# A graph network on one core: what a gather waits for on TensorE, in the attention and at the two passages between layers

## The chip, the core and the metric

The kernel runs on one core of a Trainium2 chip. The metric is device time in microseconds (us) from start to end of one execution, lower is better. The core has four engines that compute (TensorE or PE, VectorE or DVE, ScalarE or ACT, GpSimd or POOL) and SyncE (SP), which issues most transfers. Each engine works through its own list of instructions in order, and waits on semaphores for the others.

## What is computed

A graph network over 6,250 nodes of 128 features and 200,000 edges that are sorted by their target node: two convolutions over the edges and then an attention over the edges. Norms, biases and the last residual are left out here:

```python
def mesh_conv(x, src, dst, ea, w1, b1, g, bt, w2, b2):
    m = jnp.concatenate([x[dst], x[src], ea], axis=-1) @ w1 + b1
    m = jax.nn.silu(group_norm(m, g, bt))
    m = m @ w2 + b2
    out = jax.ops.segment_sum(m, dst, num_segments=n)
    return out / jnp.clip(cnt, 1.0)[:, None]
...
h = mesh_conv(x, src, dst, edge_attr, c1_w1, ...)
...
h = mesh_conv(h, src, dst, edge_attr, c2_w1, ...)
...
q, k, v = h @ qw + qb, h @ kw + kb, h @ vw + vb
logits = (q[dst] * k[src]).sum(-1) * scale + (edge_attr @ ew + eb)
pe = jnp.exp(logits - segment_max(logits, dst)[dst])
w = pe / segment_sum(pe, dst)[dst]
o = jax.ops.segment_sum(w[:, :, None] * v[src], dst, num_segments=n)
```

Everything with `[dst]` is done with one-hot matrices on TensorE, because the edges are sorted by `dst`. Everything with `[src]` is a gather of rows from a table in DRAM.

## The kernel before

**Tiles and chunks.** 128 edges make a tile and TPC = 8 tiles a chunk; each of the three layers goes over NCH = 196 chunks, numbered here from 0 in the order of work (that is from the last nodes to the first; chunk 195 has three tiles). A gather (`indirect_dma_start` in `gather`, L796) is one instruction on POOL for one tile: it fetches 128 rows, of `b_d` in a convolution (128 numbers each), of `kv_d` in the attention (256 numbers, the key and the value). A chunk takes eight.

**The steps of a layer.** `pipeline` (L893) writes out step n of a layer. It fetches chunk n + 2 (`ahead` = 2): SP's loads of its node rows `pk` and of the indices `rel`, and POOL's eight gathers. Then it does the first half of chunk n and the second half of such earlier chunks as are due. In a convolution L1252 are the products of a chunk (TensorE), L1259 adds the gathered rows (DVE), and L1291 sums over the edges (TensorE). In the attention L1521 are the products `qe`, L1536 multiplies them with the gathered keys (DVE, where a chunk's logits begin), L1595 weights the gathered values (DVE, the last reader of a chunk's buffer), and L1602 sums. Logits are treated in runs: of four chunks first, then of eight. For a run of eight nothing but logits is done in the steps of its chunks; the maxima (L1569) and the weighting follow in the steps after. So chunks 4 to 11 are weighted from step 12 on, and in steps 8 to 11 there are logits alone.

**Buffers.** A convolution has four buffers for gathered rows. The attention has eleven, `gs`: three (`ge`) early ones, seven `g` and one `gl`; chunk c uses the buffer of chunk c - 11.

**What holds a gather.** Besides its buffer and its table, the first gather of a chunk may be held until TensorE has got to a place: `kept.seen` names the last TensorE instruction that had been written out when the chunk was fetched (`last_product`), and `held` makes the gather wait for it. In step n that is the last product of step n - 1, which in the attention are the products of chunk n. `fetched` leaves out the first fetch of a layer. In the attention that first fetch is chunk 2, which gathers nothing there, so chunk 3 is held:

```python
kept.seen = last_product() if fetched else None
new = ks[n + ahead] = stage.fetch(n + ahead)
kept.seen, fetched = None, True
```

**The passages between layers.** A layer's table is written by the layer before it, a batch of nodes at a time, and the last tile of nodes is ready only after the last edge sums (`last_tile`). The first EARLY = 3 chunks of convolution 2 and of the attention therefore gather from a copy (`b_e`, `kv_e`) that lacks this last tile. They do so while the layer before is still ending, and what they lack is added later with one-hot matrices `ohS` and the rows in `late` (L1700 and L1702 in the attention). Chunk 3 is the first that reads the complete table. In `last_tile` L972 are transpositions, L990 products and L1080 the stores of the last rows.

**Order on an engine.** DVE, SP, ACT and PE keep the order of the text, and POOL's gathers follow each other in the order in which they are written (`follows`). `ring` semaphores (`ring_r1` and so on) let the t-th gather of a chunk wait for the t-th of the chunk before.

Of the kernel before, what the change touches and what calls it, by code (L numbers as in the profile page):

```python
# [31 lines left out]
TPC = 8  # L32
# [6 lines left out]
EARLY = 3  # L39
# [18 lines left out]
def kernel(ctx: ExitStack, tc: tile.TileContext, x, src, dst, eat, w, out):  # L58
# [29 lines left out]
    kept = SimpleNamespace(h0=hpc.tile([P, NW, D], FP, name="h0"))  # L88
# [80 lines left out]
    b_d = {i: dram.tile([NW * P, D], FP, name=f"b_d{i}") for i in (1, 2)}  # L169
    kv_d = dram.tile([NW * P, KV], FP, name="kv_d")  # L170
    b_e = dram.tile([NW * P, D], FP, name="b_e")
    kv_e = dram.tile([NW * P, KV], FP, name="kv_e")
# [72 lines left out]
    with tc.tile_pool(name="node0", bufs=1) as np_, tc.tile_pool(name="prep", bufs=1) as pp, \  # L245
# [99 lines left out]
        back, firsts = sums[:, :NCH], sums[:, 2 * P:2 * P + NCH]  # L345
# [445 lines left out]
            tc.add_to_no_dep_group(key, h.ins)  # L791

    def gather(k, g, table_d, ring=None):
        n = k.nt
        for t in range(n):
            h = nc.gpsimd.indirect_dma_start(  # L796
                out=g[:, t, :table_d.shape[1]], out_offset=None, in_=table_d,
                in_offset=bass.IndirectOffsetOnAxis(ap=k.src[:, t:t + 1], axis=0))
            if ring is None:
                continue  # L800
            if kept.behind is not None:
                follows(h, kept.behind)
            kept.behind = h.ins
            if t == 0 and kept.seen is not None:
                held(h, kept.seen)
            ring.mark(h, k.at, t, n - 1)

    kept.behind = kept.seen = None

    def last_product():  # L810
        return next((i.name for i in reversed(nc.cur_bb.bb.instructions) if i.engine == mybir.EngineType.PE), None)

    def held(h, name):
        tc.add_manual_dep(
            h.ins, name, mybir.DependencyInfo(mybir.DependencyClass.Sync, mybir.DependencyReason.DATA),
            reason="held until TensorE is there")
# [76 lines left out]
    def pipeline(i, stage, following=None, aside=iter(()), then=iter(())):  # L893


        ends, todo = steps_of(i)
        starts = {n: j for j, (n, _, _) in enumerate(plans[i])}
        ahead = stage.ahead
        ks, under_way, said, fetched = stage.ks, [], {}, False

        def go_on(n, those):
            for g in those:
                if said.get(g) == "held" and n + 1 in ends:
                    continue
                said[g] = next(g, STOP)
                if said[g] is STOP:
                    under_way.remove(g)

        for c in range(ahead):
            if c not in ks:  # L910
                ks[c] = stage.fetch(c)
                compared(ks[c])
        stage.products(ks[0])
        for n, seconds in enumerate(todo):
            new = None
            if n + ahead < NCH and n + ahead not in ks:
                kept.seen = last_product() if fetched else None
                new = ks[n + ahead] = stage.fetch(n + ahead)
                kept.seen, fetched = None, True
            elif following and n + ahead >= NCH:  # L920
                kept.seen = last_product()
                new = following.prefetch(n + ahead - NCH)
                kept.seen = None
            if n + 1 < NCH and stage.soon:
                stage.products(ks[n + 1])
            run = [ks[c] for c in ends.get(n, ())]
            stage.root(run)
            early = stage.soon and n > NCH - SOON
            if early:
                ahead_of = [g for g in under_way if said.get(g) not in ("var", "root")]  # L930
                go_on(n, ahead_of)
            if new and stage.soon:
                compared(new)
            first = (lambda k: lambda: stage.first(k))(ks[n]) if n < NCH else None
            stage.then = [ks[c] for c in (todo[n + 1] if n + 1 < len(todo) else ()) if c in ks]
            if stage.second(run, [ks.pop(c) for c in seconds], first) and first:
                first()
            stage.finish()
            if new and not stage.soon:
                compared(new)  # L940
            if n + 1 < NCH and not stage.soon:
                stage.products(ks[n + 1])
            if n + 1 < len(todo):
                stage.early(ks, n, todo[n + 1])
            if n in starts:
                for _ in aside:
                    pass
                under_way.append(stage.batch(starts[n]))
            go_on(n, [g for g in under_way if not early or g not in ahead_of])
            if n > 4 and next(aside, STOP) is STOP and n > min(starts):  # L950
                next(then, None)
            if n < NCH:
                stage.reduce(ks[n])
        stage.flush()
        for g in (*under_way, aside, then):
            for _ in g:
                pass
# [206 lines left out]
    def nodes_of(b, i, w, m, hx=None):  # L1164
        return attention_nodes(b, w, m, hx) if i == 3 else conv_nodes(b, i, w, m, last=hx is not None)
# [22 lines left out]
    def last_tile(b, i, hx=True):  # L1188

        slots, b.bank = b.bank(), None  # L1190
        turn = itertools.cycle(range(BN))

        def slot():
            j = next(turn)
            return slots[:, j:j + 1, :]

        b.bank = slot
        b.var = lambda: last_var
        b.rs = last_rs
        nc.scalar.activation(last_sd[:, :1], eps_t, AF.Sqrt)  # L1200
        for r in nodes_of(b, i, 0, 1, hx):
            if r == "root":
                nc.scalar.activation(last_sd, last_var, AF.Sqrt, bias=eps_t, scale=1.0 / HD)  # L1203
            if r == ("inverse" if i == 3 else "root"):
                nc.vector.reciprocal(last_rs, last_sd)  # L1205
# [10 lines left out]
    def convs(general=False):  # L1216
        with ExitStack() as es:
            pool = lambda n, b, **kw: es.enter_context(tc.tile_pool(name=f"{n}{'g' if general else 'c'}", bufs=b, **kw))
            pools = {"oh": pool("oh", 2), "ps": pool("ps", 1, space=PSUM)}
            if not general:  # L1220
                pools["ohT"] = pool("ohT", 2)
                ring = Ring("ring", GB)
# [75 lines left out]

            class Stage:
                ahead, soon = 2, True  # L1300

                def __init__(self, i):
                    self.i, self.ks = i, {}
# [10 lines left out]
                def fetch(self, c):  # L1314
                    k = chunk(self.i, c)
                    loads(k, self.pools, a_d[self.i], wc_d[self.i])
                    k.g = gp.tile([P, TPC, D], FP, name="g")
                    gather(k, k.g, b_d[self.i] if k.ohS is None else b_e, ring)
                    k.h = hs[c % len(hs)]
                    return k  # L1320

# [144 lines left out]
    gs = [None] * (G + 3)  # L1466

    class AheadOfAttention:

        @staticmethod  # L1470
        def prefetch(c):
            k = chunk(3, c)
            gather(k, gs[c], kv_e, ring3)

    ahead_of = AheadOfAttention()

    def attention(general=False):
# [197 lines left out]

        class Stage:
            ahead, soon = 2, False
            sums, late, nb = [], [], None
            lg, j, both = None, 0, None

# [128 lines left out]
        if not general:  # L1809
            stage = Stage()  # L1810
# [127 lines left out]
```

## Time and profile before

| | |
|---|---|
| median of 3 runs | 6007.2 us (6005.33 to 6008.46) |
| the profiled execution | 6010.35 us, span 6008.6 us |
| convolution 1's gathers, from | 39.95 us |
| convolution 2's first early gather | 2002.8 us |
| the attention's first early gather | 3960.9 us |
| the attention's first gather of the complete table | 4011.5 us |
| the last gather | 5951.6 us |
| mean granted clock of TensorE | 0.746 |

The span goes from the first instruction to the last; the rest of an execution's time lies around it. In the rows of the timeline the first number is the start in us from the span's start, the second the duration; in brackets stands the idle time of the engine just before, and what ended it. In the groups and in the views of one line the numbers behind the bar or the colon are busy time and mean, or the least, the median and the largest duration in ns; what follows is idle time by releaser. In the view of waits they are the sum in us, how often, and the longest. "issue" is time in which the engine waited for nothing that the profile shows. POOLq is POOL's sequencer, which takes instructions up ahead of the engine itself.

### The profile page before, as it was taken

The numbers are of one execution on the slowest core, as the hardware profiler recorded it, in microseconds if no ns is written. First come the engines' busy times: TensorE is split into PE (matmuls) and PEld (weight loads), VectorE is DVE, ScalarE is ACT, GpSimd is POOL, SyncE is SP. The second block draws the span as 40 slices with busy tenths as digits, with TensorE's granted clock in tenths as the row PEclk, the third lists the DMA queues.
The fourth block names the chain that finished last, engine by engine and source line by source line (L and its number), as shares of the span: only waits on it lengthen the run. The fifth ranks groups of instructions, "written<-read, shape, count | busy, mean of one in ns | idle before, by whom it ended". The sixth has DMA issues, their size and how long they took to land. (4 is left out here: it accounts for less than half of the span.)

```text
span 6008.6 us, 66534 instructions
## 1 busy us (share of the span) xinstructions
PE 3651.7 (61%) x20680; PEld 3461.7 (58%) x20681; DVE 4879.3 (81%) x6840; ACT 3324.6 (55%) x5207; POOL 4503.0 (75%) x4763
## 2 busy tenths in 40 slices
PE   6665555555555665555566655555666666666665
PEld 5555555555555555555555555555666565666565
DVE  7888888888888777777888888856787788888876
ACT  5666666666666666666666666642333333333574
POOL 7777777777777777777777777767777777777775
PEclk7667777777777777777777777867777777777777
DMA  5333333333333323233333333334444455555553
GB/s 158 90 108 100 80 87 89 91 92 89 91 92 88 81 78 81 78 82 78 83 98 99 100 98 102 102 86 137 137 135 136 135 140 144 142 147 138 147 143 84
DMA packets 384005, 640.81 MB, mean 107 GB/s; under 512 B 91184, under 2 KB 249628, under 8 KB 382059
## 3 DMA queue, kind: packets, MB, share of 16 engines
q0 software_dynamic: 175056, 410.03, 25.9%
q1 hardware_dynamic: 205482, 225.32, 13.1%
q8 instruction: 167, 2.74, 0.2%
q14 instruction: 196, 1.61, 0.1%
q10 hardware_dynamic: 3104, 1.12, 0.1%
HBM read 588.95 MB, written 47.17 MB: 106 GB/s over the span
## 5 line engine op out<-in xcount | busy, mean ns | idle before, releaser
L796 POOL DMA_INDIRECT g<-b_d,src_i x3102 | 2944.8, 949 | 951.6 <-issue 924.7
L1291 PE MATMUL u<-h,oh 128*128 128x129 f32 (+1 forms) x6252 | 1330.0, 399 | 1514.5 <-ACT h L1283 1514.5
L1291 PEld LDWEIGHTS u<-h,oh 128*128 128x128 f32 x6252 | 1229.3, 302 | 1590.9 <-ACT h L1283 1590.9
L796 POOL DMA_INDIRECT g<-kv_d,src_i x995 | 944.5, 949 | 333.9 <-issue 311.9
L1252 PE MATMUL m<-pk,ohT 101*128 101x128 f32 x6252 | 918.9, 309 | 63.7 <-DVE h L1259 44.3
L1252 PEld LDWEIGHTS m<-pk,ohT 101*128 101x128 f32 x6252 | 898.1, 228 | 75.7 <-DVE h L1259 53.7
L1259 DVE TENSOR_TENSOR h<-m,g 128x1024 f32<-128x1024 f32 x392 | 475.9, 1214 | 570.7 <-DMA g<-b_d,src_i 535.1
L1521 PE MATMUL qe<-pk,ohT 101*128 101x136 f32 x3126 | 595.6, 365 | 349.2 <-ACT ebs L1538 341.3
L1602 PE MATMUL us<-v,oh 128*128 128x145 f32 x3126 | 610.3, 366 | 294.1 <-DVE flat L1627 206.7
L1521 PEld LDWEIGHTS qe<-pk,ohT 101*128 101x128 f32 x3126 | 551.4, 263 | 383.9 <-ACT ebs L1538 375.5
L1602 PEld LDWEIGHTS us<-v,oh 128*128 128x128 f32 x3126 | 564.9, 256 | 337.4 <-DVE flat L1627 160.9
L1261 ACT ACTIVATE sq<-h 128x1024 f32<-128x1024 f32 x392 | 412.8, 1053 | 569.4 <-DVE h L1259 567.8
L1283 ACT ACTIVATE h<-h 128x1024 f32<-128x1024 f32 (+2 forms) x394 | 413.2, 1049 | 558.9 <-DVE h L1282 543.1
L763 ACT ACTIVATE ohT<-rel,minus_p 96x1024 f32<-96x1024 bf16 x588 | 668.7, 1137 | 16.8 <-DMA rel<-rel_d 8.6
L764 ACT ACTIVATE ohT<-ohT 96x1024 f32<-96x1024 f32 x588 | 619.9, 1054 | 19.2
L1263 DVE TENSOR_REDUCE var<-sq 128x64 f32<-128x1024 f32 x392 | 473.9, 1209 | 25.5 <-ACT sq L1261 25.1
L1281 DVE TENSOR_TENSOR h<-h,cps 128x1024 f32<-128x1024 f32 (+2 forms) x394 | 477.4, 1212 | 13.5
L1282 DVE TENSOR_TENSOR h<-h,cps 128x1024 f32<-128x1024 f32 (+2 forms) x394 | 477.4, 1212 | 13.5
L796 POOL DMA_INDIRECT ge<-kv_d,src_i x408 | 388.6, 952 | 124.3 <-issue 119.4
L1278 DVE TENSOR_TENSOR h<-h,cps 128x1024 f32<-128x1024 f32 (+2 forms) x394 | 474.5, 1204 | 0.8
L827 DVE TENSOR_TENSOR oh<-cps,dm 128x1024 f32<-128x1024 f32 x392 | 474.3, 1210 | 0.7 <-PE u L1291 0.6
L1615 ACT ACTIVATE us<-d 128x16 f32<-128x16 f32 x172 | 32.1, 187 | 602.6 <-DVE d L1611 435.2
(294 smaller groups left out, 4459.9 us busy)
## 6 DMA issues: line engine op xcount, KB each, us to landing
rel<-rel_d SPq DMA_DIRECT2D x291, 384.0 KB
g<-b_d,src_i POOLq DMA_INDIRECT x3102, 2.6
pk<-a_d SPq DMA_DIRECT2D x588, 46.0 KB
g<-kv_d,src_i POOLq DMA_INDIRECT x995, 2.8
ohT<-in_eat_dram SPq DMA_DIRECT2D x291, 40.0 KB
ge<-kv_d,src_i POOLq DMA_INDIRECT x408, 2.8
a_d<-n_o SPq DMA_DIRECT2D x24, 256.0 KB
kv_d<-n_o SPq DMA_DIRECT2D x24, 256.0 KB
```

Source lines behind the costliest of these rows:

```text
L763: nc.scalar.activation(k.ohT[:WN, :], k.rel, AF.Square, bias=minus_p[:WN])
L764: nc.scalar.activation(k.ohT[:WN, :], k.ohT[:WN, :], AF.Relu, bias=1.0, scale=-4.0)
L796: h = nc.gpsimd.indirect_dma_start(out=g[:, t, :table_d.shape[1]], out_offset=None, in_=table_d, in_offset=bass.IndirectOffsetOnAxis(ap=k. ...
L827: return nc.vector.tensor_tensor(k.oh[:, :k.nt, :], iota[:, None, :].to_broadcast([P, k.nt, P]), k.dm[:, :, None].to_broadcast([P, k.nt, P ...
L1252: nc.tensor.matmul(k.m[:, t, :], lhsT=lhs[:, t * P:(t + 1) * P], rhs=rhs, start=(j == 0), stop=(j == len(terms) - 1))
L1259: nc.vector.tensor_tensor(k.mt, k.m[:, :n], k.g[:, :n], ALU.add)
L1278: nc.vector.tensor_tensor(m4, m4, k.rs.rearrange("p (t g) -> p t g", g=H)[:, a:a + n, :, None].to_broadcast([P, n, H, HD]), ALU.mult)
L1281: nc.vector.tensor_tensor(mt, mt, over_edges(gam, n), ALU.mult)
L1282: nc.vector.tensor_tensor(mt, mt, over_edges(bet, n), ALU.add)
L1291: nc.tensor.matmul(k.u[:, 0, :wide(k)], lhsT=k.oh[:, t, :], rhs=k.h[:, t, :wide(k)], start=start and t == 0, stop=stop and t == k.nt - 1)
L1521: nc.tensor.matmul(k.qe[:, t // TB, at:at + DB], lhsT=lhs[:, t * P:(t + 1) * P], rhs=rhs, start=(j == 0), stop=(j == len(terms) - 1))
L1602: nc.tensor.matmul(k.u[:, :wide], lhsT=k.oh[:, t, :], rhs=k.v[:, t, :wide], start=(t == 0), stop=(t == k.nt - 1))
```

## The change

A gather of a layer's loop is held by the place that TensorE had reached `lag` steps further back, and the fetches of chunks up to EARLY = 3 are not held in the loop at all. The convolutions have a lag of 0. The attention has 3 for chunks under 12, 2 for 12 and 13, and 1 from 14 on. Where n - lag is below zero there is no hold, which is so for chunk 4 of the attention. `marks` keeps the places. Second, chunk 2 of convolution 2 and of the attention, the last early one, comes in two halves of four gathers: the first is written out at the end of the loop of the layer before and held by the last TensorE instruction there, the second inside `last_tile`, behind the seventh of its pieces, and held by the last TensorE instruction there. What is computed stays the same.

```diff
--- before.py
+++ after.py
@@ -791,8 +791,16 @@
             tc.add_to_no_dep_group(key, h.ins)
 
     def gather(k, g, table_d, ring=None):
+        for _ in gathered(k, g, table_d, ring):
+            pass
+
+    def gathered(k, g, table_d, ring, halves=False):
+
         n = k.nt
         for t in range(n):
+            if halves and t % (TPC // 2) == 0:
+                yield
+                kept.seen = last_product()
             h = nc.gpsimd.indirect_dma_start(
                 out=g[:, t, :table_d.shape[1]], out_offset=None, in_=table_d,
                 in_offset=bass.IndirectOffsetOnAxis(ap=k.src[:, t:t + 1], axis=0))
@@ -801,11 +809,17 @@
             if kept.behind is not None:
                 follows(h, kept.behind)
             kept.behind = h.ins
-            if t == 0 and kept.seen is not None:
+            if (t == 0 or halves) and kept.seen is not None:
                 held(h, kept.seen)
+                kept.seen = None
             ring.mark(h, k.at, t, n - 1)
-
-    kept.behind = kept.seen = None
+        yield
+
+    def early_gather(c, *what):
+        kept.rest = gathered(*what, c == EARLY - 1)
+        next(kept.rest)
+
+    kept.behind = kept.seen = kept.rest = None
 
     def last_product():
         return next((i.name for i in reversed(nc.cur_bb.bb.instructions) if i.engine == mybir.EngineType.PE), None)
@@ -896,7 +910,7 @@
         ends, todo = steps_of(i)
         starts = {n: j for j, (n, _, _) in enumerate(plans[i])}
         ahead = stage.ahead
-        ks, under_way, said, fetched = stage.ks, [], {}, False
+        ks, under_way, said, marks = stage.ks, [], {}, []
 
         def go_on(n, those):
             for g in those:
@@ -913,10 +927,12 @@
         stage.products(ks[0])
         for n, seconds in enumerate(todo):
             new = None
+            marks.append(last_product())
             if n + ahead < NCH and n + ahead not in ks:
-                kept.seen = last_product() if fetched else None
+                back = n - stage.lag(n + ahead)
+                kept.seen = marks[back] if n + ahead > EARLY and back >= 0 else None
                 new = ks[n + ahead] = stage.fetch(n + ahead)
-                kept.seen, fetched = None, True
+                kept.seen = None
             elif following and n + ahead >= NCH:
                 kept.seen = last_product()
                 new = following.prefetch(n + ahead - NCH)
@@ -951,6 +967,8 @@
                 next(then, None)
             if n < NCH:
                 stage.reduce(ks[n])
+        if following:
+            next(kept.rest)
         stage.flush()
         for g in (*under_way, aside, then):
             for _ in g:
@@ -1198,7 +1216,9 @@
         b.var = lambda: last_var
         b.rs = last_rs
         nc.scalar.activation(last_sd[:, :1], eps_t, AF.Sqrt)
-        for r in nodes_of(b, i, 0, 1, hx):
+        for n, r in enumerate(nodes_of(b, i, 0, 1, hx)):
+            if i < 3 and n == 6:
+                next(kept.rest)
             if r == "root":
                 nc.scalar.activation(last_sd, last_var, AF.Sqrt, bias=eps_t, scale=1.0 / HD)
             if r == ("inverse" if i == 3 else "root"):
@@ -1298,6 +1318,7 @@
 
             class Stage:
                 ahead, soon = 2, True
+                lag = staticmethod(lambda c: 0)
 
                 def __init__(self, i):
                     self.i, self.ks = i, {}
@@ -1315,7 +1336,10 @@
                     k = chunk(self.i, c)
                     loads(k, self.pools, a_d[self.i], wc_d[self.i])
                     k.g = gp.tile([P, TPC, D], FP, name="g")
-                    gather(k, k.g, b_d[self.i] if k.ohS is None else b_e, ring)
+                    if k.ohS is None:
+                        gather(k, k.g, b_d[self.i], ring)
+                    else:
+                        early_gather(c, k, k.g, b_e, ring)
                     k.h = hs[c % len(hs)]
                     return k
 
@@ -1470,7 +1494,7 @@
         @staticmethod
         def prefetch(c):
             k = chunk(3, c)
-            gather(k, gs[c], kv_e, ring3)
+            early_gather(c, k, gs[c], kv_e, ring3)
 
     ahead_of = AheadOfAttention()
 
@@ -1675,6 +1699,7 @@
 
         class Stage:
             ahead, soon = 2, False
+            lag = staticmethod(lambda c: 3 if c < 12 else 2 if c < 14 else 1)
             sums, late, nb = [], [], None
             lg, j, both = None, 0, None
```

The same instructions stand on POOL in the same order, and on the other engines nothing differs; what differs is what gathers wait for.

The first place is POOL at the passage from convolution 2 to the attention: the gathers of the last early chunk (`ge`, from `kv_e`) and the first one of chunk 3 (`g`, from `kv_d`). PE_49, DVE_49 and Activation_49 are counts of those engines' work, DMAHW of SP's transfers, DMASW of gathers. Before:

```order
L796 DMA ge_5561<-kv_e,src_i 128x256
L796 DMA ge_5561<-kv_e,src_i 128x256 [waits ring3_r1]
L796 DMA ge_5561<-kv_e,src_i 128x256 [waits ring3_r2]
L796 DMA ge_5561<-kv_e,src_i 128x256 [waits ring3_r3]
L796 DMA ge_5561<-kv_e,src_i 128x256 [waits ring3_r4]
L796 DMA ge_5561<-kv_e,src_i 128x256 [waits ring3_r5]
L796 DMA ge_5561<-kv_e,src_i 128x256 [waits ring3_r6]
L796 DMA ge_5561<-kv_e,src_i 128x256
L796 DMA g_22588<-kv_d,src_i 128x256 [waits DMAHW3_49,DMAHW5_49,DMAHW1_49,DMAHW6_49,DMAHW0_49,DMAHW7_49,PE_49,Pool_49]
```

Now:

```order
L804 DMA ge_5561<-kv_e,src_i 128x256 [waits PE_49]
L804 DMA ge_5561<-kv_e,src_i 128x256 [waits ring3_r1]
L804 DMA ge_5561<-kv_e,src_i 128x256 [waits ring3_r2]
L804 DMA ge_5561<-kv_e,src_i 128x256 [waits ring3_r3]
L804 DMA ge_5561<-kv_e,src_i 128x256 [waits PE_49,ring3_r4]
L804 DMA ge_5561<-kv_e,src_i 128x256 [waits ring3_r5]
L804 DMA ge_5561<-kv_e,src_i 128x256 [waits ring3_r6]
L804 DMA ge_5561<-kv_e,src_i 128x256
L804 DMA g_22588<-kv_d,src_i 128x256 [waits DMAHW5_49,DMAHW3_49,DMAHW6_49,DMAHW1_49,DMAHW7_49,DMAHW0_49,Pool_49]
```

The first and the fifth gather of the early chunk have got a wait for PE, and the gather of chunk 3 has lost its wait for PE; its waits for transfers are the same six.

The second place is POOL from the end of chunk 3 to chunk 5 of the attention. Before:

```order
L796 DMA g_22588<-kv_d,src_i 128x256 [waits ring3_r6]
L796 DMA g_22588<-kv_d,src_i 128x256
L796 DMA g_22589<-kv_d,src_i 128x256 [waits PE_49]
L796 DMA g_22589<-kv_d,src_i 128x256 [waits ring3_r1]
L796 DMA g_22589<-kv_d,src_i 128x256 [waits ring3_r2]
L796 DMA g_22589<-kv_d,src_i 128x256 [waits ring3_r3]
L796 DMA g_22589<-kv_d,src_i 128x256 [waits ring3_r4]
L796 DMA g_22589<-kv_d,src_i 128x256 [waits ring3_r5]
L796 DMA g_22589<-kv_d,src_i 128x256 [waits ring3_r6]
L796 DMA g_22589<-kv_d,src_i 128x256 [waits DMASW4_49]
L796 DMA g_22590<-kv_d,src_i 128x256 [waits DVE_49,PE_49,Activation_49]
```

Now:

```order
L804 DMA g_22588<-kv_d,src_i 128x256 [waits ring3_r6]
L804 DMA g_22588<-kv_d,src_i 128x256
L804 DMA g_22589<-kv_d,src_i 128x256
L804 DMA g_22589<-kv_d,src_i 128x256 [waits ring3_r1]
L804 DMA g_22589<-kv_d,src_i 128x256 [waits ring3_r2]
L804 DMA g_22589<-kv_d,src_i 128x256 [waits ring3_r3]
L804 DMA g_22589<-kv_d,src_i 128x256 [waits ring3_r4]
L804 DMA g_22589<-kv_d,src_i 128x256 [waits ring3_r5]
L804 DMA g_22589<-kv_d,src_i 128x256 [waits ring3_r6]
L804 DMA g_22589<-kv_d,src_i 128x256 [waits DMASW4_49]
L804 DMA g_22590<-kv_d,src_i 128x256 [waits DVE_49,PE_49,Activation_49]
```

Chunk 4's first gather (the third row) has lost its wait for PE. Chunk 5's (the last row) keeps one: before for chunk 3's products, now for chunk 0's, as the lag of 3 says.

The third place is POOL at chunk 3 of convolution 1. Before:

```order
L796 DMA g<-b_d_100,src_i 128x128 [waits ring_r4]
L796 DMA g<-b_d_100,src_i 128x128 [waits ring_r5]
L796 DMA g<-b_d_100,src_i 128x128 [waits ring_r6]
L796 DMA g<-b_d_100,src_i 128x128
L796 DMA g<-b_d_100,src_i 128x128 [waits PE_49]
L796 DMA g<-b_d_100,src_i 128x128 [waits ring_r1]
```

Now:

```order
L804 DMA g<-b_d_100,src_i 128x128 [waits ring_r4]
L804 DMA g<-b_d_100,src_i 128x128 [waits ring_r5]
L804 DMA g<-b_d_100,src_i 128x128 [waits ring_r6]
L804 DMA g<-b_d_100,src_i 128x128 x2
L804 DMA g<-b_d_100,src_i 128x128 [waits ring_r1]
```

The first gather of chunk 3 has lost its wait for PE, so that its row reads like the one ahead of it and is counted with it.

## The prediction

> **What bounds the kernel now.** I read the page's busy line first, then POOL's groups, then the waits, then POOL's rows in order of time.
>
> ```profile
> span 6008.6 us, 66534 instructions
> PE 3651.7 (61%) x20680; PEld 3461.7 (58%) x20681; DVE 4879.3 (81%) x6840; ACT 3324.6 (55%) x5207; POOL 4503.0 (75%) x4763
> L796 POOL DMA_INDIRECT g<-b_d,src_i x3102 | 2944.8, 949 | 951.6 <-issue 924.7
> L796 POOL DMA_INDIRECT g<-kv_d,src_i x995 | 944.5, 949 | 333.9 <-issue 311.9
> ```
>
> DVE looks busiest, but POOL's idle is nearly all "issue": a gather is followed by about 0.30 us in which it waits for nothing. Gather and gap together take 1.25 us, eight of them about 10 us a chunk. Whether POOL or the engines that use the rows set the pace is told by the waits:
>
> ```profile
> DVE h L1259 <- DMA g<-b_d,src_i: 535.1, 257, 8.3
> DVE g L1536 <- DMA g<-kv_d,src_i: 133.5, 62, 6.9
> DVE ge L1536 <- DMA ge<-kv_d,src_i: 63.1, 30, 7.2
> DVE gl L1536 <- DMA gl<-kv_d,src_i: 27.5, 11, 7.2
> ```
>
> DVE stands 535 us in the convolutions and 133.5 + 63.1 + 27.5 = 224 us in the attention for rows that have not landed. So POOL's chain of gathers is the bound, and a stall in it moves the end one for one as long as DVE has some of those 224 us left behind it. Between its first gather and its last, POOL's timeline has just five rows with over half a us of idle time; they stand here, with the row ahead of the second:
>
> ```profile
> 72.69 0.94 POOL L796 DMA_INDIRECT g<-b_d,src_i  x1 [1.05 <-PE m L1252]
> 3989.72 0.95 POOL L796 DMA_INDIRECT ge<-kv_e,src_i  x1 [0.30 <-issue]
> 4011.50 0.94 POOL L796 DMA_INDIRECT g<-kv_d,src_i  x1 [20.84 <-issue]
> 4024.36 0.94 POOL L796 DMA_INDIRECT g<-kv_d,src_i  x1 [3.16 <-PE qe L1521]
> 4038.15 0.94 POOL L796 DMA_INDIRECT g<-kv_d,src_i  x1 [4.09 <-issue]
> 5949.05 0.94 POOL L796 DMA_INDIRECT g<-kv_d,src_i  x1 [3.90 <-PE qe L1521]
> ```
>
> They are the first gathers of chunk 3 of convolution 1 (72.69), of chunks 3, 4 and 5 of the attention (4011.50 to 4038.15) and of its last chunk, 195 (5949.05). Two are labelled "issue", but TensorE's rows and those of POOL's sequencer show the hold in them:
>
> ```profile
> 4006.74 4.00 PE L1521 MATMUL qe<-pk,ohT 101*128 101x136 f32 x16 [3.00 <-ACT ebs L1538]
> 4033.60 3.79 PE L1521 MATMUL qe<-pk,ohT 101*128 101x136 f32 x16 [3.00 <-ACT ebs L1538]
> L796 POOLq EVENT_SEMAPHORE  x2: 5203/14704/24205, 3981.3 to 3986.6; - x2
> ```
>
> Chunk 1's products end at 4010.74, chunk 3's at 4037.39; the held gathers start 0.76 us after each. Of the two semaphore waits the first runs from 3981.3 for 5.2 us, to 3986.5, and the second from 3986.6 for 24.2 us, to 4010.8: the table's writes had mostly landed by 3986.5, and what remained was TensorE.
>
> **The change part by part.** *Attention, chunk 3.* Its hold on the products of chunk 1 is gone; what stays is the wait for the writes of kv_d, which SP issued from 3983.06 on:
>
> ```profile
> 3983.06 1.56 SPq L1080 DMA_DIRECT2D kv_d<-late  x2
> ```
>
> POOL's last early gather begins at 3989.72 and ends at 3990.67. If the writes have landed by then, chunk 3 starts at 3990.97, with the usual 0.30: 20.84 - 0.30 = 20.54 us saved. *Chunk 4* is no longer held: 3.16 - 0.30 = 2.86. *Chunk 5* is now held by chunk 0's products, of step 0 and not 3; these are done before chunk 1's at 4006.74, and the gather would come at 4011: 4.09 - 0.30 = 3.79. *Chunks 6 to 11* are held three steps further back. Chunk 8 is the tightest: it wants to start at 3990.97 + 5 x 10.0 = 4041, and its products (chunk 3's) end at 4037.39. *Convolution 1, chunk 3*: 1.05 - 0.30 = 0.75. *Chunk 195* starts 3.6 us earlier, and I count it at nothing, since its rows are used far later:
>
> ```profile
> 5973.52 0.51 DVE L1536 TENSOR_TENSOR g<-qe,g 128x384 f32<-128x384 f32 x1
> ```
>
> That is 21 us after the gather's end; if the cover were gone it would be worth up to 3.6. *All other chunks of the attention* wait for a TensorE step one further back, at a place where POOL does not wait at all: nothing.
>
> *The halves.* Here waits are added: on chunk 2's first and fifth gather, at both passages. Behind them on POOL stands chunk 3 of the next layer. The first half waits for the last sums (L1291), the second for the transposition of n_A (L972):
>
> ```profile
> 2012.16 4.79 PE L1291 MATMUL u<-h,oh 128*128 128x129 f32 x22 [6.91 <-ACT h L1283]
> 2021.35 0.47 PE L972 MATMUL nd<-ident,n_A 128*128 128x128 f32 x1 [2.00 <-DVE n_A L1001]
> 2022.79 0.94 POOL L796 DMA_INDIRECT g<-b_e,src_i  x1 [0.30 <-issue]
> 2027.78 0.94 POOL L796 DMA_INDIRECT g<-b_e,src_i  x1 [0.30 <-issue]
> 3970.94 5.00 PE L1291 MATMUL u<-h,oh 128*128 128x128 f32 x22 [7.22 <-ACT h L1283]
> 3979.90 0.47 PE L972 MATMUL nd<-ident,n_A 128*128 128x128 f32 x1 [1.23 <-DVE n_A L1001]
> 3980.97 0.95 POOL L796 DMA_INDIRECT ge<-kv_e,src_i  x1 [0.30 <-issue]
> 3985.97 0.95 POOL L796 DMA_INDIRECT ge<-kv_e,src_i  x1 [0.30 <-issue]
> ```
>
> TensorE is there at 2016.95 and 2021.82, POOL comes at 2022.79 and 2027.78; in the second passage 3975.94 and 3980.37 against 3980.97 and 3985.97. The margins are 5 to 6 us and a hold passed on in 0.76 us above, so the halves move nothing. Without that cover they would cost what TensorE is late by.
>
> *What POOL's new start runs into.* After the passage POOL is 20.54 + 2.86 + 3.79 = 27.19 us ahead. Two things must follow: DVE has to catch up, and a buffer must be free when the gather comes. DVE's rows:
>
> ```profile
> 4031.89 1.29 DVE L1536 TENSOR_TENSOR ge<-qe,ge 128x768 f32<-128x768 f32 x2
> 4037.42 1.29 DVE L1536 TENSOR_TENSOR g<-qe,g 128x768 f32<-128x768 f32 x2 [2.66 <-PE qe L1521]
> 4041.77 1.29 DVE L1536 TENSOR_TENSOR g<-qe,g 128x768 f32<-128x768 f32 x2 [1.48 <-PE qe L1521]
> 4061.21 1.29 DVE L1536 TENSOR_TENSOR g<-qe,g 128x768 f32<-128x768 f32 x2
> 4069.79 1.29 DVE L1536 TENSOR_TENSOR g<-qe,g 128x768 f32<-128x768 f32 x2 [1.01 <-DMA g<-kv_d,src_i]
> 4079.96 1.29 DVE L1536 TENSOR_TENSOR g<-qe,g 128x768 f32<-128x768 f32 x2 [3.69 <-DMA g<-kv_d,src_i]
> 4119.81 1.29 DVE L1536 TENSOR_TENSOR ge<-qe,ge 128x768 f32<-128x768 f32 x2 [7.20 <-DMA ge<-kv_d,src_i]
> 4130.13 1.22 DVE L1595 TENSOR_TENSOR v<-g,pe 128x1024 f32<-128x1024 f32 x1 [0.38 <-ACT v L1591]
> 4138.12 0.94 POOL L796 DMA_INDIRECT g<-kv_d,src_i  x1 [0.30 <-issue]
> ```
>
> Chunks 2 to 4 (4031.89, 4037.42, 4041.77) are not bound by gathers, chunks 7 and 8 (4069.79, 4079.96) and on to 12 (4119.81) are. Without those waits chunk 7 comes at 4068.78 and chunk 8 at 4079.96 - 1.01 - 3.69 = 4075.26. From there four light steps lead to chunk 12. Such a step took 4.35 us (4037.42 to 4041.77) or 5.53 us (4031.89 to 4037.42), so chunk 12 comes at 4092.7 or 4097.4. Chunk 15's gather reuses the buffer of chunk 4, which is read last by L1595: it ends at 4131.35, 11.54 us after chunk 12's start, so now at 4104.2 or 4108.9. POOL wants that buffer at 4138.12 - 27.19 = 4110.93. It is free in both, by 6.7 or 2.0 us: no wait. Chunk 12 needs rows that POOL brings by 4119.81 - 27.19 = 4092.6, so DVE is again at POOL's heels some chunks later, and from there on everything is 27.19 us earlier.
>
> For the two prices of a light step: the slower one held 3.79 us of products behind a TensorE idle of 3.00 us, in the faster one they took 2.61 behind 1.74.
>
> ```profile
> 4039.13 2.61 PE L1521 MATMUL qe<-pk,ohT 101*128 101x136 f32 x16 [1.74 <-ACT ebs L1538]
> ```
>
> The Trainium skill has a rule that speaks against the change here ("TensorE: Matmul & The Clock Gate", "Part 1: The HAM clock gate"): TensorE's clock is halved after an idle window of some 3.4 us. By it light steps with idle between them would all have the slow price; the rows agree as far as they go, and the sum by that rule stays the same, with 2.0 us of margin in place of 6.7.
>
> *The sum.* 20.54 + 2.86 + 3.79 + 0.75 = 27.94 us. The profiled execution took 6010.35 us around its span of 6008.6; 6010.35 - 27.94 = 5982.4. The median of the runs shown, 6007.2, lies 3.15 below that execution, so I forecast 6007.2 - 27.9 = 5979.3 us.
>
> **The rivals.** *A wait for the buffer takes the hold's place.* If the light steps take as long as the longest one that the rows show without gather waits (4061.21 to 4069.79, less 1.01: 7.57 us), chunk 12 comes at 4105.5 and the buffer is free at 4117.1. POOL then stands 6.1 us, the gain is 21.8 and the time 5985.4. For it: three of four steps of that kind are unseen. Against it: that step also carried the weighting and merging of another chunk, which steps 8 to 11 do not.
>
> *The change doesn't do what it says for chunk 3.* The long semaphore wait also held one write of the table. If that write, or a reuse of memory, is what ended at 4010.8, chunk 3 stays at 4011.50 and 20.54 are lost: 2.86 + 3.79 + 0.75 = 7.4 us, 5999.8. Against it: the wait ended within 0.1 us of the products of chunk 1.
>
> *Slower: a gather costs more once POOL runs further ahead.* Its place is L796 in the attention, some 1,540 gathers. To eat 27.9 us and 12 more, one must take 40 / 1540 = 26 ns longer, so it decides from a mean of about 975 ns. At 980 ns the loss is 48 - 28 = 20 us: 6027. Against it, two mid-kernel groups, one of a convolution (100 to 2000 us) and one of the attention (4100 to 5700 us), have the same mean. The third row, of DVE from 4160 to 5720 us, is for the sentence behind:
>
> ```profile
> L796 POOL DMA_INDIRECT g<-b_d,src_i x1515 | 1438.4, 949 | 461.7 <-issue 452.9 <-DVE h L1282 3.7 <-PE m L1252 2.1
> L796 POOL DMA_INDIRECT g<-kv_d,src_i x806 | 764.5, 949 | 245.5 <-issue 232.1 <-DVE d L1612 4.0 <-PE us L1602 1.8
> L1613 DVE COPY M<-mn 128x16 f32 x157 | 30.6, 195 | 0.9 <-DVE d L1612 0.9
> ```
>
> The Trainium skill names a mechanism for it ("SBUF — State Buffer", "SBUF: two separate sides"): while VectorE runs a copy that takes two ports, GpSimd cannot write a DMA's descriptors. The attention has such copies (L1613) and the trace shows no price for them.
>
> **How the numbers follow.** The forecast gets 0.70 (gain 25 to 31: 5976 to 5982), the buffer's wait 0.16 (5982 to 5991), the unmoved chunk 3 0.10 (5999.8), the slower gather 0.04. About 0.2%, 12 us, is what a measurement of this kernel tells from no change. The first two are faster by more than that, 0.86; the third is within it, 0.10; slower 0.04. The range goes from 5975 (chunk 195's 3.6 us counted, and half a us of scatter) to 5990, which takes in all of the first case and most of the second.
>
> **What would show it.** In POOL's timeline chunk 3 of the attention starts near 3990.2 with 0.30 us of idle, and no idle over 0.5 us stands before chunk 195. DVE's waits for kv_d fall by some 27 us, and chunks 8 to 12 lose theirs. The halves show 0.30. A gap on POOL at chunk 15 or 16 would be the first rival; a long POOLq wait that ends near 4010, the second; a mean of L796 above 960 ns, the third. I am wrong if POOL's rows move as said and the end does not: then DVE or TensorE, and not POOL, set the attention's end.

## The result, and the profile after

| | before | after |
|---|---|---|
| median | 6007.3 us (5 runs, 6005.33 to 6008.91) | 5977.13 us (5 runs, 5973.42 to 5977.49) |
| the profiled execution | 6010.35 us, span 6008.6 us | 5977.49 us, span 5975.8 us |
| the attention's first early gather | 3960.94 us | 3957.32 us |
| the attention's chunk 3 | 4011.50 us | 3987.35 us |
| the attention's chunk 15 | 4138.12 us | 4107.41 us |

The change makes the kernel faster by half a per cent: ratio 0.9949, 95% interval 0.9936 to 0.9962. That is 30.2 us by the medians, where 27.9 were forecast. In the new kernel the lines have moved: the gathers are now L804, the attention's products L1545, the start of its logits L1560, the weighting L1619.

The page of the changed kernel, its busy line and POOL's two largest groups:

```profile
span 5975.8 us, 66536 instructions
PE 3636.1 (61%) x20680; PEld 3445.5 (58%) x20681; DVE 4878.3 (82%) x6840; ACT 3322.9 (56%) x5207; POOL 4502.5 (75%) x4763
...
L804 POOL DMA_INDIRECT g<-b_d,src_i x3102 | 2943.2, 949 | 951.0 <-issue 918.0
...
L804 POOL DMA_INDIRECT g<-kv_d,src_i x995 | 945.9, 951 | 303.1 <-issue 286.7
```

A gather costs what it did (949 and 951 ns; 949 and 949 before). What went is idle time in front of the second group: 333.9 us before, 303.1 now. POOL's rows of the changed kernel show from where; the first number is the start, the second the duration, the bracket the idle time before:

```profile
38.78 1.17 POOL L804 DMA_INDIRECT g<-b_d,src_i  x1 [5.87 <-DMA b_d<-b]
...
3986.10 0.94 POOL L804 DMA_INDIRECT ge<-kv_e,src_i  x1 [0.30 <-issue]
3987.35 0.95 POOL L804 DMA_INDIRECT g<-kv_d,src_i  x1 [0.30 <-issue]
...
3997.36 0.95 POOL L804 DMA_INDIRECT g<-kv_d,src_i  x1 [0.31 <-issue]
...
4007.36 0.95 POOL L804 DMA_INDIRECT g<-kv_d,src_i  x1 [0.30 <-issue]
...
4107.41 0.94 POOL L804 DMA_INDIRECT g<-kv_d,src_i  x1 [0.30 <-issue]
...
5915.58 1.00 POOL L804 DMA_INDIRECT g<-kv_d,src_i  x1 [0.30 <-issue]
5916.88 0.95 POOL L804 DMA_INDIRECT g<-kv_d,src_i  x1 [0.30 <-issue]
5918.13 0.95 POOL L804 DMA_INDIRECT g<-kv_d,src_i  x1 [0.30 <-issue]
```

Chunks 3, 4, 5, 15 and 195 of the attention (the rows with 3987.35 to 5915.58) follow the gather ahead of them after the usual 0.30 us. From its first gather to its last, POOL has no idle of half a us left: 4,689 gathers in 5919.08 - 38.78 = 5880.3 us are 1.254 us each. That is the time of the new kernel but for its start and its tail.

DVE's waits for rows, in the changed kernel's view of waits (sum in us, how often, the longest):

```profile
DVE h L1279 <- DMA g<-b_d,src_i: 550.4, 267, 7.3
DVE g L1560 <- DMA g<-kv_d,src_i: 123.9, 67, 4.1
DVE ge L1560 <- DMA ge<-kv_d,src_i: 47.2, 27, 3.5
DVE gl L1560 <- DMA gl<-kv_d,src_i: 22.1, 9, 4.3
```

In the attention they are 193.2 us in sum, against 224.1: DVE had 31 us less to wait and still waits. POOL is the bound as before.

### The profile page after: what moved, and what is told of

It reads as the page before. It is cut to its first block, busy times and chain, and to the rows that moved or that the text cites. A ratio compares the mean times of both kernels' runs of the same rounds, so it can differ in the third digit from the quotient of the medians.

```text
span 5975.8 us, 66536 instructions
## 1 busy us (share of the span) xinstructions
PE 3636.1 (61%) x20680; PEld 3445.5 (58%) x20681; DVE 4878.3 (82%) x6840; ACT 3322.9 (56%) x5207; POOL 4502.5 (75%) x4763
## 5 line engine op out<-in xcount | busy, mean ns | idle before, releaser
L804 POOL DMA_INDIRECT g<-b_d,src_i x3102 | 2943.2, 949 | 951.0 <-issue 918.0
L804 POOL DMA_INDIRECT g<-kv_d,src_i x995 | 945.9, 951 | 303.1 <-issue 286.7
L1545 PE MATMUL qe<-pk,ohT 101*128 101x136 f32 x3126 | 580.4, 358 | 332.0 <-ACT ebs L1562 323.9
L1545 PEld LDWEIGHTS qe<-pk,ohT 101*128 101x128 f32 x3126 | 536.5, 257 | 366.2 <-ACT ebs L1562 357.4
L1283 DVE TENSOR_REDUCE var<-sq 128x64 f32<-128x1024 f32 x392 | 473.8, 1209 | 21.2 <-ACT sq L1281 20.8
L804 POOL DMA_INDIRECT ge<-kv_d,src_i x408 | 388.3, 952 | 124.3 <-issue 117.6
```

The costliest lines, as they stand in the source:

```text
L804: h = nc.gpsimd.indirect_dma_start(out=g[:, t, :table_d.shape[1]], out_offset=None, in_=table_d, in_offset=bass.IndirectOffsetOnAxis(ap=k. ...
L1545: nc.tensor.matmul(k.qe[:, t // TB, at:at + DB], lhsT=lhs[:, t * P:(t + 1) * P], rhs=rhs, start=(j == 0), stop=(j == len(terms) - 1))
```

## Experiments

**First chip, the lag alone.** Four kernels are the change with one line put otherwise; everything else of it stays, the free start of chunk 3 among it. They ask whether each removed wait is worth its length by itself, or whether only the last hold counts.

```diff
-            lag = staticmethod(lambda c: 3 if c < 12 else 2 if c < 14 else 1)
+            lag = staticmethod(lambda c: 0)                     # e1_lag0
+            lag = staticmethod(lambda c: 1)                     # e2_lag1
+            lag = staticmethod(lambda c: 2 if c < 14 else 1)    # e3_lag2
+            lag = staticmethod(lambda c: NCH)                   # e4_noholds
```

e1_lag0, expected:

> Chunk 3 of the attention is free as in the change, all later chunks are held where the kernel before held them. If each hold has a price of its own that adds up, 20.54 us of chunk 3 and 0.75 of convolution 1 are won: about 21.3 us below the kernel before. If a hold is a point in time that TensorE sets, the hold of chunk 5 (chunk 3's products, which the new start of POOL does not move) decides alone: chunk 4 starts where it did, behind some 23.7 us of idle, chunk 5 behind 4.1, and only 0.75 us is won, which is no change that can be measured.

e2_lag1, expected:

> A lag of 1 in all of the attention. If prices add up chunk by chunk, the three stalls of before are gone and the gain is the change's, 28 to 30 us. If holds are points in time, the tightest is chunk 6 behind chunk 3's products: it starts 0.76 us after them, where the kernel before started chunk 5; chunk 6 is then one chunk, 10.0 us, earlier, so 10.0 + 0.75 = 10.8 us in all, and idle stands on POOL before chunks 4, 5 and 6.

e3_lag2, expected:

> A lag of 2 up to chunk 13. Adding up: 28 to 30 us. Points in time: chunk 7 starts 0.76 us after chunk 3's products, two chunks earlier than before: 20.0 + 0.75 = 20.8 us, with short idle before chunks 5, 6 and 7.

e4_noholds, expected:

> No hold at all on chunks 3 to 195 of the attention; buffers, tables and the order of gathers remain. Points in time: a lag of 3 already let POOL run without idle, so the time is the change's (within 2 us) and POOL's rows are the same. If the holds that remain in the change protect something (loads of SP that gathers would crowd out, buffers), it is slower than the change by over 3 us, with idle before chunk 15 where the buffer of chunk 4 is reused.

The kernel before took 6001.3 us on this chip.

| | median | ratio, 95% interval |
|---|---|---|
| e1_lag0 | 6002.47 us | 1.0002 (0.9993 to 1.0011) |
| e2_lag1 | 5990.83 us | 0.9982 (0.9973 to 0.9991) |
| e3_lag2 | 5980.63 us | 0.9968 (0.9956 to 0.998) |
| e4_noholds | 5977.19 us | 0.9961 (0.9947 to 0.9975) |

By the reading that holds are points in time, e1, e2 and e3 were to gain 0.75, 10.8 and 20.8 us on the kernel before. Measured are -1.2 (no change that can be told), 10.5 and 20.7. The reading by which each wait has a price of its own gave 21.3 and twice 28 to 30, and falls.

POOL's timeline tells why. e1_lag0, chunks 3, 4 and 5 of the attention:

```profile
3988.80 0.95 POOL L804 DMA_INDIRECT g<-kv_d,src_i  x1 [0.30 <-issue]
...
4021.25 0.94 POOL L804 DMA_INDIRECT g<-kv_d,src_i  x1 [22.75 <-PE qe L1545]
...
4035.07 0.94 POOL L804 DMA_INDIRECT g<-kv_d,src_i  x1 [4.12 <-issue]
```

Chunk 3 is free, as in the change, and starts without a wait. Yet nothing is won: chunk 4, still held by products of TensorE that come when they come, now waits 22.75 us in place of 3.16, and chunk 5 waits 4.12, as before. e2_lag1, chunks 4, 5 and 6:

```profile
4004.08 0.94 POOL L804 DMA_INDIRECT g<-kv_d,src_i  x1 [9.35 <-PE qe L1545]
...
4016.60 0.94 POOL L804 DMA_INDIRECT g<-kv_d,src_i  x1 [2.83 <-issue]
...
4029.15 0.94 POOL L804 DMA_INDIRECT g<-kv_d,src_i  x1 [2.85 <-PE qe L1545]
```

e3_lag2, chunks 5, 6 and 7:

```profile
4006.97 0.94 POOL L804 DMA_INDIRECT g<-kv_d,src_i  x1 [0.47 <-issue]
...
4019.73 0.94 POOL L804 DMA_INDIRECT g<-kv_d,src_i  x1 [3.08 <-PE qe L1545]
...
4032.98 0.94 POOL L804 DMA_INDIRECT g<-kv_d,src_i  x1 [3.55 <-PE qe L1545]
```

With every step of lag the last hold that POOL still meets passes on a chunk later and ends sooner, measured against a chain of 10.0 us a chunk. A removed wait has no price of its own: what counts is how late the last held gather starts. Without any hold (e4_noholds) POOL takes 150.06 us from its first early gather to chunk 15, and 150.09 in the change, so on a chip like this one the lag of 3, 2 and 1 that the change keeps costs nothing.

**Second chip.** The next four kernels came to a chip on which the kernel before takes 6972.15 us. They were meant to price the halves, the all-through part and the buffers.

e5_whole, the change with chunk 2 gathered in one piece:

```diff
     def early_gather(c, *what):
-        kept.rest = gathered(*what, c == EARLY - 1)
+        kept.rest = gathered(*what)
         next(kept.rest)
...
-        if following:
-            next(kept.rest)
...
-            if i < 3 and n == 6:
-                next(kept.rest)
```

> The change with the last early chunk in one piece, not held, as before. My reading: TensorE was 5 to 6 us ahead of both halves, so the time is the change's, within 2 us. If the halves carry the 2 us that the change gained above the forecast, this one lies 2 to 3 us above the change, near 5979.5 us.

e6_halves, the halves with the holds as before:

```diff
-        ks, under_way, said, marks = stage.ks, [], {}, []
+        ks, under_way, said, marks, fetched = stage.ks, [], {}, [], False
...
-                back = n - stage.lag(n + ahead)
-                kept.seen = marks[back] if n + ahead > EARLY and back >= 0 else None
+                kept.seen = marks[n] if fetched else None
...
-                kept.seen = None
+                kept.seen, fetched = None, True
```

> The kernel before with the halves alone; all other holds are as before. My reading: no change, 6007 us within 2 us, the long idle before chunk 3 still there. If the halves carry something: 2 to 3 us below the kernel before.

e7_late0, the change with the holds from chunk 14 on as before:

```diff
-            lag = staticmethod(lambda c: 3 if c < 12 else 2 if c < 14 else 1)
+            lag = staticmethod(lambda c: 3 if c < 12 else 2 if c < 14 else 0)
```

> The change with a lag of 0 from chunk 14 on, so without the step back all through. My reading: the time of the change within 2 us, one gap of about 3.9 us on POOL, before chunk 195. If the end of the kernel did gain from chunk 195's earlier start, it lies 2 to 3.6 us above the change.

e8_ten, ten buffers in the attention: `gs` has G + 2 entries and `gl` is gone. In step 12 the fetch of chunk 14, which then takes chunk 4's buffer, is written out ahead of chunk 4's weighting. So what it computes is not the reference's attention, and its time does not tell what a wait for that buffer would cost.

> The change with ten buffers for gathered rows in the attention and not eleven, so that chunk 14 reuses chunk 4's buffer. My reading of the buffer's wait: in the change that buffer is free 3.9 us before chunk 15 wants it, and chunk 14 wants it 10.0 us earlier, so POOL stands about 6.1 us before chunk 14; at the later runs of eight the margin of 10 to 11 us falls to about 0 to 1, so there at most some tenths each. In all 6 to 9 us above the change. If buffers are no limit so early: the time of the change.

| | median | ratio, 95% interval |
|---|---|---|
| e5_whole | 7212.62 us | 1.034 (1.0326 to 1.0354) |
| e6_halves | 6958.85 us | 0.9981 (0.9972 to 0.9991) |
| e7_late0 | 6962.6 us | 0.9984 (0.9975 to 0.9993) |
| e8_ten | 7012.36 us | 1.005 (1.0036 to 1.0063) |

These times don't settle the expectations, because the chain of gathers is another one here. A convolution of e6_halves, POOL's rows, with the 16 gathers between the two waits left out but for the first and the last:

```profile
1008.30 0.94 POOL L804 DMA_INDIRECT g<-b_d,src_i  x1 [2.63 <-remote]
...
1027.39 0.94 POOL L804 DMA_INDIRECT g<-b_d,src_i  x1 [0.30 <-issue]
1031.13 0.94 POOL L804 DMA_INDIRECT g<-b_d,src_i  x1 [2.80 <-remote]
```

A gather takes 0.94 us and 0.30 between two as on the first chip, but here POOL stands some 3 us after 16 of them, and what ends the wait is not in the core's own records ("remote"): 1031.13 - 1008.30 = 22.83 us for 16, where the first chip needs 16 x 1.25 = 20.0. Of the 114 distances between POOL's waits of over half a us in this convolution 68 are 16 gathers, 40 are 8 and 6 are 24, so all of them stand where a chunk begins. The pause is not POOL's alone. VectorE and ScalarE come out of a wait of the same label 0.23 us ahead of POOL:

```profile
1030.90 1.22 DVE L1278 TENSOR_TENSOR h<-m,g 128x1024 f32<-128x1024 f32 x1 [5.77 <-remote]
1030.90 0.72 ACT L1315 ACTIVATE u<-u,mask 128x129 f32<-128x129 f32 x2 [4.68 <-remote]
```

What all three wait for is not shown. No trace shows the kernel before on this chip; as an estimate, 4,689 gathers with 2.83 us for every 16 would be some 830 of the 965 us that it takes longer here.

The holds that the change keeps are not free here. Chunks 6, 7 and 8 of the attention in e7_late0:

```profile
4642.58 0.95 POOL L804 DMA_INDIRECT g<-kv_d,src_i  x1 [11.26 <-PE qe L1545]
4655.85 0.94 POOL L804 DMA_INDIRECT g<-kv_d,src_i  x1 [3.58 <-PE qe L1545]
4669.10 0.94 POOL L804 DMA_INDIRECT g<-kv_d,src_i  x1 [3.55 <-PE qe L1545]
```

From the first early gather to chunk 15 it takes 200.13 us, and e6_halves, with the holds as before, 198.39: the 27 us that the first chip gains on this way are not there. e6_halves lies 13.3 us below the kernel before and clear of it, though nothing was expected; why is open. The change itself was not among these runs, so that e5, e7 and e8 can't be set against it.

e5_whole is a surprise even so, 254 us above e6_halves. The idle in front of the attention's gathers, from the pages of the two; e5_whole:

```profile
L804 POOL DMA_INDIRECT g<-kv_d,src_i x995 | 945.7, 950 | 702.2 <-issue 271.1
...
L804 POOL DMA_INDIRECT ge<-kv_d,src_i x408 | 388.3, 952 | 287.0 <-issue 110.9
```

and e6_halves:

```profile
L804 POOL DMA_INDIRECT g<-kv_d,src_i x995 | 946.5, 951 | 552.1 <-issue 265.8
...
L804 POOL DMA_INDIRECT ge<-kv_d,src_i x408 | 389.6, 955 | 223.9 <-issue 108.4
```

(702.2 + 287.0) - (552.1 + 223.9) = 213 of the 254 us lie there, with gathers of some 950 ns in both. Most of the 254 us comes late: from chunk 15's first gather to the last gather it takes 2362.0 us in e5_whole and 2136.0 in e6_halves. Why the attention falls into a slower rhythm in one of these kernels and not in the others was not settled; it needed runs of the change on such a chip.

**Third chip, the parts again.** The change, e5, e6 and e7 were therefore run once more, together; this chip is like the first, with the kernel before at 6005.54 us.

e9_change, expected:

> The change itself, beside three of its parts on one chip. On the chip of e5 to e8, where the kernel before takes 6972 us and each 16th gather is followed by a pause of about 3.25 us on POOL, the change has not run; its own time there is missing, so e5 to e8 cannot be set against it. If this chip is like the first one (kernel before at 6001 to 6010): ratio 0.995 to 0.996, 24 to 30 us under the kernel before. If it is like the second (before at about 6970): the theory of the prediction, which takes the gathers' chain as the only limit, makes it some 10 us faster, as e7_late0 was (9.5); a rival, that the order of the gathers' holds matters there in another way, makes it as slow as e5_whole (+240).

e10_whole (the edit of e5_whole), expected:

> The change with the last early chunk gathered in one piece, as before. By the prediction the halves are worth nothing (each half has 5 to 6 us to spare before its reader): within 6 us of e9_change on a chip like the first. Rival: the halves are what lets the attention's chunks move up, since the whole chunk 2 stands in POOL's queue ahead of chunk 3; then it would lose a part of the 27 us: 10 us or more above e9_change. On a chip like that of e5 it was 240 us above the kernel before; if that is the halves' doing, e9_change does not show it, and if it is the chip's doing with the holds one step further back, e9_change shows it too.

e11_halves (the edit of e6_halves), expected:

> The holds as before and the halves alone. By the prediction nothing: within 6 us of the kernel before on a chip like the first. Rival (the halves carry a part of the gain): 10 us or more below it. On the chip of e5 it was 13 us below.

e12_late0 (the edit of e7_late0), expected:

> The change with the hold of attention chunks 14 to 195 put back to where it was before (behind the products of the step itself), so without its all-through part. By the prediction this part is worth nothing but the one wait of 3.9 us at chunk 195, which had 21 us to spare: within 6 us of e9_change. Rival, that the later holds carry a part of the gain: 10 us or more above e9_change. A second rival, that a hold kept later spreads the gathers better: below e9_change by 6 us or more.

| | median | ratio, 95% interval |
|---|---|---|
| e9_change | 5977.93 us | 0.9958 (0.9944 to 0.9971) |
| e10_whole | 5977.18 us | 0.9957 (0.9944 to 0.9971) |
| e11_halves | 6007.42 us | 0.9999 (0.999 to 1.0008) |
| e12_late0 | 5977.91 us | 0.9959 (0.9945 to 0.9972) |

On this chip the halves alone win nothing, leaving them out loses nothing, and the later holds are worth nothing either way. e10_whole passes from the last early gather to chunk 3 like the change:

```profile
3985.53 0.95 POOL L804 DMA_INDIRECT ge<-kv_e,src_i  x1 [0.30 <-issue]
3986.78 0.95 POOL L804 DMA_INDIRECT g<-kv_d,src_i  x1 [0.30 <-issue]
```

e11_halves, chunks 3, 4 and 5, has the three old waits, only that chunk 3's is 1.2 us longer:

```profile
4012.11 0.94 POOL L804 DMA_INDIRECT g<-kv_d,src_i  x1 [22.07 <-issue]
...
4024.86 0.94 POOL L804 DMA_INDIRECT g<-kv_d,src_i  x1 [3.06 <-PE qe L1544]
...
4038.59 0.94 POOL L804 DMA_INDIRECT g<-kv_d,src_i  x1 [4.04 <-issue]
```

**All of it in one table.** From POOL's timelines: the attention's first early gather, the first gather of its chunk 15, behind the last of the short-lived holds, and the way between them, in us.

| | first | chunk 15 | way |
|---|---|---|---|
| before | 3960.94 | 4138.12 | 177.18 |
| e11_halves | 3960.38 | 4138.58 | 178.20 |
| e1_lag0 | 3958.84 | 4135.03 | 176.19 |
| e2_lag1 | 3955.08 | 4119.13 | 164.05 |
| e3_lag2 | 3956.78 | 4112.97 | 156.19 |
| the change | 3957.32 | 4107.41 | 150.09 |
| e9_change | 3959.75 | 4109.83 | 150.08 |
| e4_noholds | 3958.03 | 4108.09 | 150.06 |
| e12_late0 | 3958.57 | 4108.63 | 150.06 |
| e10_whole | 3956.81 | 4106.71 | 149.90 |

The kernels' times follow the last column: above the change's way by 26.1, 14.0 and 6.1 us, e1, e2 and e3 took 25.3, 13.6 and 3.4 us longer than e4. 15 chunks of 10.0 us are 150, so the lower end of the column is a chain without a hole.

## Why the prediction was right

**The bound.** Right. DVE kept 193 us of waits for rows in the attention after a gain of 27 there, and POOL's chain is now without holes.

**The three terms of the attention's start.** 20.54 + 2.86 + 3.79 = 27.19 us were forecast; the way from the first early gather to chunk 15 went from 177.18 to 150.09, which is 27.09. The table's writes had landed when chunk 3 came (3987.35, 0.30 idle), so the rival in which they hold it falls; e1_lag0 shows the same at 3988.80. The prediction's working has this start at 3990.97 and its list of signs at 3990.2; it came earlier because POOL reached the passage 3.62 us earlier (3957.32 against 3960.94).

What was not right is the look of this sum. It reads as if chunk 3's hold were worth 20.54 us and each of the others its own length. In the attention e1_lag0 removes chunk 3's alone and gains nothing (ratio 1.0002). The holds are points in time, not costs: only the last one that POOL meets counts, and the terms may be added because the change takes all three away.

**Convolution 1, chunk 3.** 0.75 forecast. From the first gather to chunk 3 it took 72.69 - 39.95 = 32.74 us before and 70.57 - 38.78 = 31.79 after, so 0.95 less.

**The halves, the holds all through, chunk 195.** Forecast at nothing. e10_whole, e11_halves and e12_late0 find nothing within what can be told. Chunk 195 came without a wait, its last row at 5918.13. e12_late0 keeps the old hold there, stands 2.50 us, and is no slower. From chunk 15's first gather to the end of the span the traces that have no such pauses take 1866.4 to 1870.5 us with that hold (the kernel before, e1, e11, e12) and 1866.6 to 1871.4 without it (e2, e3, e4, e9, e10 and the change): its removal can't be seen at the end.

**The buffer.** Forecast free by 6.7 or 2.0 us when chunk 15 wants it. DVE's rows of the changed kernel, logits of chunks 8 to 12 and then the weighting of chunk 4, the last reader:

```profile
4069.78 1.29 DVE L1560 TENSOR_TENSOR g<-qe,g 128x768 f32<-128x768 f32 x2
...
4074.73 1.29 DVE L1560 TENSOR_TENSOR g<-qe,g 128x768 f32<-128x768 f32 x2 [2.08 <-PE qe L1545]
...
4080.47 1.29 DVE L1560 TENSOR_TENSOR gl<-qe,gl 128x768 f32<-128x768 f32 x2 [2.81 <-PE qe L1545]
...
4086.20 1.29 DVE L1560 TENSOR_TENSOR ge<-qe,ge 128x768 f32<-128x768 f32 x2 [2.86 <-PE qe L1545]
...
4091.93 1.29 DVE L1560 TENSOR_TENSOR ge<-qe,ge 128x768 f32<-128x768 f32 x2 [2.86 <-PE qe L1545]
...
4102.24 1.22 DVE L1619 TENSOR_TENSOR v<-g,pe 128x1024 f32<-128x1024 f32 x1 [0.37 <-ACT v L1615]
```

The weighting ends at 4103.46, chunk 15's gather starts at 4107.41: free by 3.95 us, no wait, and the first rival falls. No wait for rows is left in these steps; DVE now waits for TensorE. One light step took 4.95 us and three took 5.73, the mean 5.54: the slower of the two prices. TensorE's rows and the windows (us, busy time and instructions of the engines, granted clock, DMA share, GB/s) of the changed kernel say why:

```profile
4072.36 2.34 PE L1545 MATMUL qe<-pk,ohT 101*128 101x136 f32 x16
4076.43 3.99 PE L1545 MATMUL qe<-pk,ohT 101*128 101x136 f32 x16 [1.74 <-ACT ebs L1562]
4082.17 3.99 PE L1545 MATMUL qe<-pk,ohT 101*128 101x136 f32 x16 [1.74 <-ACT ebs L1562]
```

```profile
4072.00:4078.00 6.00, 4.26 (x26) 4.06 (x25) 3.33 (x6) 3.38 (x6) 4.48 (x6) 0.78 0.37 105
4078.00:4084.00 6.00, 4.26 (x19) 3.94 (x19) 2.73 (x4) 2.63 (x5) 4.48 (x6) 0.50 0.62 187
4084.00:4090.00 6.00, 4.26 (x19) 3.94 (x19) 2.73 (x4) 2.61 (x5) 4.48 (x6) 0.50 0.41 115
```

The granted clock falls to 0.50 and the same 16 products take 3.99 us in place of 2.34. So the half clock was there, and the margin came out between the two that were forecast, not closed. That it is 3.95 and not the 2.0 of the slow price lies ahead of these steps: chunk 8 began at 4069.78, 5.48 us before the time worked out for it (4075.26), and POOL was only 3.52 us before its own (4107.41 against 4110.93). One reading of the prediction is wrong here: it says that its rows agree with the rule of the Trainium skill ("TensorE: Matmul & The Clock Gate", "Part 1: The HAM clock gate"), an idle window of some 3.4 us, but the idle times in those rows are 3.00 and 1.74 us, both shorter.

**A slower gather.** 949 and 951 ns, far from the 975 at which this rival began.

**The size.** 30.2 us by the medians against 27.9. By the two profiled executions the gain is 32.86: 27.09 on the way above and 0.95 in convolution 1, which are the forecast's parts, and 4.8 outside: 1.2 ahead of the first gather, 1.5 in the rest of the way to the attention and 2.1 from chunk 15 to the end. Kernels that are alike in these parts scatter by as much: the attention's first gather lies between 3955.08 and 3959.75 in the table's runs of kernels that start chunk 3 freely. In the experiments without the pauses the change (e9) gained 27.6 us and its like (e4) 24.1. The forecast lies within this, and how near the median came to it is in part luck.

## What to carry to other kernels

A hold on another engine's progress is a point in time. Moving or removing one gains only up to the next one that the same queue meets, so list them in order, with the time at which each opens, and ask which opens last against the pace of the queue; the wait's length in the profile is no price. When all of them lie ahead of the pace, the rest of their fine tuning, here the halves and the lags from chunk 14 on, is worth nothing. That holds for one pace only: on the second chip the same lag of 3 stopped POOL for 11.26 us.

Edits are compared with each other only within one chip. On a chip that paces the same queue in another way, a variant that gained 0.4% elsewhere lost 3.4% (e10_whole and e5_whole).

## What the runs showed of the hardware

TensorE's granted clock went to 0.50 and stayed there through steps in which it worked 3.99 us and idled 1.74. The Trainium skill ("TensorE: Matmul & The Clock Gate", "Part 1: The HAM clock gate") gives an idle window of about 3.4 us for the half clock. The halving itself agrees with these rows; the length doesn't, since no idle time ahead of these products was longer than 1.74 us from 4050 us on. In the changed kernel the clock was 1.00 from 4060 to 4069 us with TensorE busy for 4.45 of the 9 us, 0.50 from 4070 to 4072 with TensorE busy throughout, 1.00 again from 4073 to 4076, and 0.50 from 4077 to 4093.

One chip had pauses of about 3 us on POOL where chunks begin, most often after 16 gathers (22.83 us for 16 in place of 20.0), and the kernel before took 16% longer there (6972.15 against 6007.3 us). A gather's own time was the same on all of them, 948 to 952 ns in the groups `g` of `b_d` and `kv_d`. What POOL, and with it VectorE and ScalarE, waits for in this pause the trace doesn't show.
